# Mamba scan in a graph network on one core: B and C rows as sums of three BF16 parts, C read from PSUM, and GpSimd making the input of five of sixteen states

## The chip, the cores and the metric

The kernel runs on one core of one Trainium2 chip. The metric is the device time of one execution in microseconds, the median of the runs shown. Beside it stands one profiled execution, whose span and records are used for all readings of the trace.

## The reference, cut to what matters

Four graph layers follow each other on a graph of 3327 nodes with 256 features, each as `x = layernorm(x + layer(x, adj))`. The change lies in layer 1: one graph convolution, and then a Mamba block whose sequence is the nodes.

```python
h = jax.nn.relu(adj @ x @ gcn_w + gcn_b)
h = layernorm(h) * ln_g + ln_b
xz = h @ w_in                                  # 256 -> 2 x 512
xc, z = xz[:, :512], xz[:, 512:]
u = silu(causal_conv4(xc, conv_w) + conv_b)
dbc = u @ w_xp                                 # 512 -> 16 (dt) + 16 (B) + 16 (C)
dt = softplus(dbc[:, :16] @ w_dt + b_dt)
B, C = dbc[:, 16:32], dbc[:, 32:]
dA  = exp(dt[:, :, None] * A)                  # A = -exp(A_log): 512 x 16
dBu = dt[:, :, None] * B[:, None, :] * u[:, :, None]
def step(hst, inp):                            # hst: 512 channels x 16 states
    dAt, dBut, Ct = inp
    hst = dAt * hst + dBut
    return hst, hst @ Ct
_, ys = lax.scan(step, 0, (dA, dBu, C))
return ((ys + u * D_skip) * silu(z)) @ w_out
```

All inputs and the output are FP32.

## The kernel before

The nodes are padded to 26 tiles of 128. Layer 0 runs first (up to some 366 us), then layer 1, then two more layers; the change touches layer 1 alone.

In layer 1 the token axis is cut into chunks of 512 columns (`WC`): six whole ones and a last one of 256. The 512 channels lie as four groups (`NG`) of 128 partitions. For each chunk and each of the 16 states `s`:

- `rows(x, s)`: for each of the two rows B and C of the state, TensorE broadcasts the row over 128 partitions, by an FP32 product of a column of the identity with `dbc` (48 rows), into a PSUM tile `ps`; ScalarE copies it to an SBUF tile `row` (L324). Then ScalarE makes `dA` by four Exp activations, one a group (L328).
- `scan(x, s)`: VectorE multiplies `du` (dt times u, 2048 columns) by the B row into `db` (L336), runs four scans of 512 columns (L339), copies the last column of each into `carry` (L341), and multiplies the result `h` by the C row (L342).
- TensorE adds `h` over the states into four PSUM tiles `y` through a product with the identity (L393).

Round these lie other pieces of work, which the loop over chunks and states mixes in:

- `convolve()`, a generator that `pump()` advances once per state: the adjacency product for one later tile in three stretches of up to nine products (L204), then its projection by `gcn_w`, Relu, `stats`, `rstd_of` (ScalarE's Sqrt and VectorE's reciprocal, L72 and L73) and `standardize` (L81). Its inner function `rest` transposes the tile and writes it into `hT`.
- `head(c + 1)`, a generator advanced in the last nine states: projections to `xc`, the causal convolution on VectorE (L270, L273), Silu, `dbc`, and softplus in pieces for `dt` and `du`.
- `gate_input(c)`, once per chunk at state 6: four projections with Silu into `sz`.
- `gate` and `back` of the chunk before, after state 0: the skip and gate products, `w_out`, the residual into `X` with statistics, and GpSimd's four scalings of `X` (L370).

The program text gives the order only in part: a scheduler places the instructions of each engine into that engine's queue, and each queue is then worked off in order. Waits are on semaphores. Tiles come from pools with a fixed number of buffers; an instruction that writes a buffer waits until its last reader is done. The pools that matter here are `ps` (three PSUM banks shared by the projections, transposes, rows and `w_out`), the PSUM pool `l1q` with one bank for `cb` (the accumulator of `convolve`), four banks for `y`, and in SBUF `row` (3), `dA` (2), `db` (1) and `h` (2).

Of the kernel before, what the change touches and what calls it, by code (L numbers as in the profile page):

```python
# [9 lines left out]
F32 = mybir.dt.float32  # L10
BF16 = mybir.dt.bfloat16
# [6 lines left out]
P = 128  # L18
D = 256
EPS = 1e-5  # L20
JH = 13
JC = 9
WC = 512
DI = 512
NG = DI // P
# [15 lines left out]
def gnn_kernel(ctx: ExitStack, tc: tile.TileContext, n: int, a: dict, out: bass.AP):  # L41
# [28 lines left out]
    def rstd_of(dst, var):  # L70
        std = small.tile([P, var.shape[1]], F32, name="std")
        nc.scalar.activation(std, var, AF.Sqrt, bias=eps_t)  # L72
        nc.vector.reciprocal(dst, std)  # L73
# [52 lines left out]
    with tc.tile_pool(name="l01", bufs=1) as xpool:  # L126
# [30 lines left out]
        with tc.tile_pool(name="l1b", bufs=1) as wpool, tc.tile_pool(name="l1aw", bufs=1) as cwork, \  # L157
                tc.tile_pool(name="l1at", bufs=2) as atp, tc.tile_pool(name="l1c", bufs=2) as ch, \
                tc.tile_pool(name="l1t", bufs=3) as tmp, tc.tile_pool(name="l1s", bufs=2) as work, \
                tc.tile_pool(name="l1p", bufs=3, space=PSUM) as psum, \  # L160
                tc.tile_pool(name="l1q", bufs=1, space=PSUM) as cpsum, \
                tc.tile_pool(name="l1y", bufs=1, space=PSUM) as ypsum:
            gw = load(wpool, "gcn_w")
# [5 lines left out]
            def by_channel(name):  # L169
# [2 lines left out]
                return t  # L172

            g1, b1 = by_channel("ln1_g"), by_channel("ln1_b")
            w_in, conv_w, conv_b, w_xp, w_dt, b_dt, d_skip, w_out, A = (
                load(wpool, x) for x in
                ("w_in", "conv_w", "conv_b", "w_xp", "w_dt", "b_dt", "D_skip", "w_out", "A_log"))

            nc.scalar.activation(A, A, AF.Exp)
            nc.vector.tensor_scalar_mul(A, A, -1.0)  # L180
# [4 lines left out]
            R = DTR + 2 * DS  # L185
            nch = -(-npad // WC)
            tw = WC // P
            hTs, us, szs = {}, {}, {}

            def scratch():  # L190
                return tmp.tile([P, NG, 3 + WC], F32, name="t")

            def convolve():

                rest = None
                for it in range(nt):
                    cb = cpsum.tile([P, 2, D], F32, name="cb")
# [17 lines left out]
                    mt = cwork.tile([P, D], F32, name="mt")  # L215
# [4 lines left out]
                    h = cwork.tile([P, D], F32, name="h")  # L220
# [32 lines left out]
            def project(c, g, w):  # L253
                ps = psum.tile([P, WC], F32, name="ps")
                for k in range(2):
                    nc.tensor.matmul(ps[:, :w], w_in[:, k, g * P:(g + 1) * P], hTs[c][:, k, :w],
                                     start=(k == 0), stop=(k == 1))
                return ps[:, :w]

            def head(c):  # L260


                w = min(WC, npad - c * WC)
                xc = scratch()
                nc.vector.tensor_copy(xc[:, :, :3], last)
# [17 lines left out]
                dbc = ch.tile([R, WC], F32, name="dbc")  # L283
                nc.scalar.copy(dbc[:, :w], ps[:R, :w])
                yield None


                v, e, e1 = (scratch()[:, :, :w] for _ in range(3))
                for g in range(NG):
                    ps = psum.tile([P, WC], F32, name="ps")  # L290
                    nc.tensor.matmul(ps[:, :w], w_dt[:, g * P:(g + 1) * P], dbc[:DTR, :w],
                                     start=True, stop=True)
                    nc.scalar.activation(v[:, g, :], ps[:, :w], AF.Identity, bias=b_dt[:, g:g + 1])
                    nc.scalar.activation(e[:, g, :], ps[:, :w], AF.Abs, bias=b_dt[:, g:g + 1])
# [11 lines left out]
                yield dbc, dt, du  # L306

            def gate_input(c):
                w = us[c].shape[2]
                sz = szs[c] = ch.tile([P, NG, WC], F32, name="sz", bufs=1)[:, :, :w]  # L310
                for g in range(NG):
                    nc.scalar.activation(sz[:, g, :], project(c, NG + g, w), AF.Silu)

            def rows(x, s):

                dbc, dt, du = x
                w = dt.shape[2]
                bc = []
                for r in (DTR + s, DTR + DS + s):
                    ps = psum.tile([P, WC], F32, name="ps")  # L320
                    nc.tensor.matmul(ps[:, :w], ident[:R, r:r + 1].to_broadcast([R, P]), dbc[:, :w],  # L321
                                     start=True, stop=True)
                    row = work.tile([P, 1, WC], F32, name="row", bufs=3)
                    nc.scalar.copy(row[:, 0, :w], ps[:, :w])  # L324
                    bc.append(row[:, :, :w].to_broadcast([P, NG, w]))
# [3 lines left out]
                return bc, dA  # L329

            def scan(x, s, bc, dA):

                du = x[2]
                w = du.shape[2]
                db = work.tile([P, NG, WC], F32, name="db", bufs=1)[:, :, :w]
                nc.vector.tensor_mul(db, du, bc[0])  # L336
                h = work.tile([P, NG, WC], F32, name="h")[:, :, :w]
                for g in range(NG):
                    nc.vector.tensor_tensor_scan(h[:, g, :], dA[:, g, :], db[:, g, :], initial=carry[:, s, g:g + 1],  # L339
                                                 op0=ALU.mult, op1=ALU.add)  # L340
                nc.vector.tensor_copy(carry[:, s, :], h[:, :, w - 1])  # L341
                nc.vector.tensor_mul(h, h, bc[1])  # L342
                return h

            def gate(c, ys):
# [7 lines left out]
            def back(c):  # L353
# [10 lines left out]
                    nc.vector.tensor_add(X[:, it, :], X0[:, it, :], po)  # L364
                    stats(mv[:, i, :], X[:, it, :])
                rs = small.tile([P, tw], F32, name="rsc")
                rstd_of(rs[:, :m], mv[:, :m, 1])
                for i in range(m):
                    it = c * tw + i
                    nc.gpsimd.tensor_scalar(X[:, it, :], X[:, it, :], mv[:, i, 0:1], rs[:, i:i + 1],  # L370
# [9 lines left out]
            for c in range(nch):  # L380
                w = us[c].shape[2]
                ahead = None
                for s in range(DS):
# [646 lines left out]
```

## Time and profile before

| | |
|---|---|
| median of 3 runs | 4333.3 us (4333.17 to 4333.75) |
| profiled execution, its own time | 4330.06 us |
| its span | 4327.9 us |
| mean granted TensorE clock | 0.927 |
| layer 1 within the span | about 366 to 1815 us |

Engines are named PE (TensorE), PEld (its weight loads), DVE (VectorE), ACT (ScalarE), POOL (GpSimd) and SP (which issues the transfers). A row of a group reads: line, engine, operation, tile written and tiles read, shape, count, then busy time in us and the mean of one in ns, then the idle time of the engine just before these instructions and what ended it. A row of a windows table reads: stretch in us, its length, busy time of PE, PEld, DVE, ACT and POOL with instruction counts, the granted clock, the busy share of the DMA engines, and GB/s. A row of a wait list reads: engine, tile and line that waited, engine, tile and line that ended it, us in total, times, longest. An FP32 product is two matmul records in the trace.

### The profile page before, as it was taken

What the parts mean: (1) busy time and instruction counts of PE and PEld (TensorE: products, weight loads), DVE (VectorE), ACT (ScalarE), POOL (GpSimd) and SP (SyncE); (2) the same over time, 40 slices, a digit from 0 to 9 for tenths busy, and PEclk for the clock granted to TensorE, in tenths of its full rate; (3) what the DMA queues carried; (4) which work ended last, traced back from release to release, by engine and by line L of the source; (5) the groups of instructions that cost most, each with busy time, mean ns of one, the idle gap of its engine ahead of it and who ended that gap; (6) DMA issues with size and microseconds to landing.
All of it is one profiled execution on the core that took longest, in us unless ns stands there. A gap on an engine that the chain in (4) does not pass through costs nothing. (4 is left out here: it accounts for less than half of the span.)

```text
span 4327.9 us, 42860 instructions
## 1 busy us (share of the span) xinstructions
PE 3880.5 (90%) x15597; PEld 2791.7 (65%) x15597; DVE 2795.9 (65%) x6159; ACT 1731.7 (40%) x2826; POOL 276.6 (6%) x344
## 2 busy tenths in 40 slices
PE   8998999999999977799889999999868889888988
PEld 7886644444444433588767777777646767676767
DVE  1111588888888899688624444444158877787784
ACT  0001444444444544510033333333265656565652
POOL 0000000000000010133300000000000000000000
PEclk9998898989898988899969999999869999999999
DMA  5443211111111000044301111111101111111111
GB/s 180 136 141 98 68 37 32 37 32 32 32 32 32 21 0 0 21 159 152 131 16 48 48 53 59 48 48 49 32 0 51 41 46 40 46 40 46 41 45 37
DMA packets 67053, 239.33 MB, mean 55 GB/s; under 512 B 8434, under 2 KB 22770, under 8 KB 66690
## 3 DMA queue, kind: packets, MB, share of 16 engines
q1 hardware_dynamic: 66818, 236.37, 17.1%
q8 instruction: 127, 2.08, 0.2%
q14 instruction: 108, 0.88, 0.1%
HBM read 232.93 MB, written 3.41 MB: 55 GB/s over the span
## 5 line engine op out<-in xcount | busy, mean ns | idle before, releaser
L393 PE MATMUL y<-h,ident 128*128 128x512 f32 (+1 forms) x896 | 466.4, 671 | 91.3 <-DVE h L342 91.3
L339 DVE TENSOR_TENSOR_SCAN h<-dA,carry,db 128x512 f32<-128x512 f32 (+1 forms) x448 | 511.6, 1193 | 4.8 <-DVE db L336 0.5
L328 ACT ACTIVATE dA<-dt,A_log 128x512 f32<-128x512 f32 (+1 forms) x448 | 281.4, 684 | 350.8 <-DVE h L339 333.1
L393 PEld LDWEIGHTS y<-h,ident 128*128 128x128 f32 x896 | 192.2, 225 | 354.2 <-issue 206.4
L204 PE MATMUL cb<-X,at 128*128 128x256 f32 x1352 | 334.6, 403 | 26.9 <-ACT h L221 14.7
L204 PEld LDWEIGHTS cb<-X,at 128*128 128x128 f32 x1352 | 270.1, 203 | 113.7 <-issue 52.2
L122 PE MATMUL acc<-Xa,wt 128*128 128x256 f32 x1352 | 322.3, 391 | 19.3 <-ACT wt L120 18.9
L122 PE MATMUL acc<-X,wt 128*128 128x256 f32 x1352 | 310.1, 383 | 10.7 <-ACT wt L120 8.7
L107 PE MATMUL acc<-xa,at 128*128 128x257 f32 x1352 | 308.3, 381 | 0.0
L107 PE MATMUL acc<-Xf,at 128*128 128x256 f32 x1352 | 307.6, 379 | 0.0
L107 PE MATMUL acc<-X,at 128*128 128x256 f32 x1352 | 304.3, 379 | 0.0
L122 PEld LDWEIGHTS acc<-Xa,wt 128*128 128x128 f32 x1352 | 260.4, 196 | 67.3 <-ACT wt L120 31.9
L642 PE MATMUL ps<-kT,q 64*128 64x416 f32 x832 | 254.8, 595 | 54.2 <-ACT e L643 31.6
L549 PE MATMUL acc<-V,at 128*128 128x257 f32 x1352 | 294.2, 379 | 1.4 <-DVE at L546 1.4
L336 DVE TENSOR_TENSOR db<-du,row 128x2048 f32<-128x2048 f32 (+1 forms) x112 | 238.9, 2133 | 82.8 <-ACT row L324 82.6
L122 PEld LDWEIGHTS acc<-X,wt 128*128 128x128 f32 x1352 | 252.4, 190 | 59.5 <-ACT wt L120 27.3
L549 PEld LDWEIGHTS acc<-V,at 128*128 128x128 f32 x1352 | 255.8, 189 | 39.8 <-DVE at L546 1.8
L107 PEld LDWEIGHTS acc<-xa,at 128*128 128x128 f32 x1352 | 255.6, 191 | 37.5 <-issue 0.7
L96 ACT COPY xt<-ps 128x256 f32<-128x256 f32 x234 | 82.0, 373 | 491.3 <-PE ps L94 436.8
L107 PEld LDWEIGHTS acc<-X,at 128*128 128x128 f32 x1352 | 253.0, 190 | 32.3
L107 PEld LDWEIGHTS acc<-Xf,at 128*128 128x128 f32 x1352 | 251.4, 190 | 31.3
L321 PE MATMUL ps<-dbc,ident 48*128 48x512 f32 (+1 forms) x448 | 234.3, 637 | 20.3 <-ACT row L324 19.8
(273 smaller groups left out, 5698.6 us busy)
## 6 DMA issues: line engine op xcount, KB each, us to landing
at<-in_adjT SPq DMA_DIRECT2D x156, 576.0 KB, 3.7
at<-in_adjT SPq DMA_DIRECT2D x104, 832.0 KB, 4.4
at<-in_adjT SPq DMA_DIRECT2D x78, 512.0 KB, 3.5
xa<-in_x SPq DMA_DIRECT2D x1, 3328.0 KB, 12.7
xt<-in_xT SPq DMA_DIRECT2D x26, 128.0 KB, 3.9
out<-h SPq DMA_DIRECT2D x25, 128.0 KB, 1.7
w_in<-in_w_in SPq DMA_DIRECT2D x1, 1024.0 KB, 5.4
U<-in_U SPq DMA_DIRECT2D x2, 512.0 KB, 6.1
```

The source lines that it names most:

```text
L96: nc.scalar.copy(t, pt)
L107: nc.tensor.matmul(acc, at[:, j, :], rhs[:, j0 + j, :], start=(j0 + j == 0), stop=(j0 + j == nt - 1))
L122: nc.tensor.matmul(acc, wt[:, j, :], rhs[:, j0 + j, :], start=(j0 + j == 0), stop=(j0 + j == nt - 1))
L204: nc.tensor.matmul(acc, at[:, j % JC, :], X0[:, j, :], start=(j == 0), stop=(j == nt - 1))
L321: nc.tensor.matmul(ps[:, :w], ident[:R, r:r + 1].to_broadcast([R, P]), dbc[:, :w], start=True, stop=True)
L328: nc.scalar.activation(dA[:, g, :], dt[:, g, :], AF.Exp, scale=A[:, g, s:s + 1])
L336: nc.vector.tensor_mul(db, du, bc[0])
L339: nc.vector.tensor_tensor_scan(h[:, g, :], dA[:, g, :], db[:, g, :], initial=carry[:, s, g:g + 1], op0=ALU.mult, op1=ALU.add)
L393: nc.tensor.matmul(ys[g][:, :w], ident, h[:, g, :], start=(s == 0), stop=(s == DS - 1))
L549: nc.tensor.matmul(acc, at[:, j, :], V[:, j0 + j, :], start=(j0 + j == 0), stop=(j0 + j == nt - 1))
L642: nc.tensor.matmul(pl[:, :w], q[a:a + DA, :], kT[a:a + DA, c0:c0 + w], start=True, stop=True)
```

## The change

- `w_xp` is loaded into `w_sp`, with the B and C columns three times over and the dt columns last, so that `dbc` comes out with 112 rows: three equal copies of B and C, then dt.
- `head` makes `parts`, 96 rows in BF16: the first 32 rows are the rounded values, the next 32 the rounded remainder, the last 32 the remainder of that. Their sum is the FP32 row. This takes two subtractions on VectorE and four copies on ScalarE, in place of one copy.
- `rows` makes the B row by a BF16 product of a 96-row selector `three` with `parts`, which sums the three parts in PSUM. Only B is copied to SBUF.
- `scan` makes the C row in the same way, into a PSUM tile `C` with one buffer, and VectorE's second product reads it there. The `ps` pool shrinks from three banks to two for that.
- `db` is made in halves of two groups (three buffers of a half). For the states 1, 4, 7, 10 and 13 GpSimd makes both halves in `rows`; for the others VectorE makes them in `scan`.
- The carry copy moves from VectorE to ScalarE.
- In layer 1 `rstd_of` is replaced by `power` on GpSimd: add eps, then pow with -0.5.
- `gate_input` does one projection in each of the states 2 to 5.
- The tiles `m`, `mt` and `h` of `convolve` share one buffer.

```diff
+POOLED = (1, 4, 7, 10, 13)
...
-                tc.tile_pool(name="l1p", bufs=3, space=PSUM) as psum, \
+                tc.tile_pool(name="l1p", bufs=2, space=PSUM) as psum, \
...
+            BC = 2 * DS
+            w_sp = wpool.tile([P, NG, 3 * BC + DTR], F32, name="w_sp")
...
+            three = wpool.tile([3 * BC, BC], BF16, name="three")
+            for k in range(3):
+                nc.sync.dma_start(w_sp[:, :, k * BC:(k + 1) * BC], a["w_xp"][:, :, DTR:])
+                nc.vector.tensor_copy(three[k * BC:(k + 1) * BC, :], ident[k * BC:(k + 1) * BC, k * BC:(k + 1) * BC])
+            nc.sync.dma_start(w_sp[:, :, 3 * BC:], a["w_xp"][:, :, :DTR])
...
+            def power(rs, var):
+                nc.gpsimd.tensor_scalar(rs, var, EPS, None, op0=ALU.add)
+                nc.gpsimd.tensor_tensor(rs, rs, mhalf[:, :var.shape[1]], op=ALU.pow)
...
-                    rstd_of(rs, mv[:, 1:2])
+                    power(rs, mv[:, 1:2])
...
-                    nc.tensor.matmul(ps[:R, :w], w_xp[:, g, :], u[:, g, :],
+                    nc.tensor.matmul(ps[:3 * BC + DTR, :w], w_sp[:, g, :], u[:, g, :],
...
-                nc.scalar.copy(dbc[:, :w], ps[:R, :w])
+                parts = ch.tile([3 * BC, WC], BF16, name="parts")[:, :w]
+                nc.scalar.copy(parts, ps[:3 * BC, :w])
+                left = scratch()[:3 * BC + DTR, 0, :w]
+                nc.scalar.copy(left, ps[:3 * BC + DTR, :w])
+                nc.vector.tensor_sub(left[:3 * BC], left[:3 * BC], parts)
+                for k in (1, 2):
+                    nc.scalar.copy(parts[k * BC:(k + 1) * BC], left[k * BC:(k + 1) * BC])
+                nc.vector.tensor_sub(parts[2 * BC:], left[2 * BC:3 * BC], parts[2 * BC:])
...
-                for r in (DTR + s, DTR + DS + s):
-                    nc.tensor.matmul(ps[:, :w], ident[:R, r:r + 1].to_broadcast([R, P]), dbc[:, :w],
-                    row = work.tile([P, 1, WC], F32, name="row", bufs=3)
-                    nc.scalar.copy(row[:, 0, :w], ps[:, :w])
+                nc.tensor.matmul(pb, three[:, s:s + 1].to_broadcast([3 * BC, P]), parts, start=True, stop=True)
+                B = work.tile([P, 1, WC], F32, name="row", bufs=2)[:, :, :w]
+                nc.scalar.copy(B[:, 0, :], pb)
...
+                dbs = [work.tile([P, 2, WC], F32, name="db", bufs=3)[:, :, :w] for _ in range(2)]
+                if s in POOLED:
+                    for i in range(2):
+                        nc.gpsimd.tensor_tensor(dbs[i], du[:, 2 * i:2 * i + 2, :], B.to_broadcast([P, 2, w]), op=ALU.mult)
...
-                nc.vector.tensor_mul(db, du, bc[0])
+                C = cpsum.tile([P, 1, WC], F32, name="C")[:, :, :w]
+                nc.tensor.matmul(C[:, 0, :], three[:, DS + s:DS + s + 1].to_broadcast([3 * BC, P]), parts,
+                                 start=True, stop=True)
+                if s not in POOLED:
+                    for i in range(2):
+                        nc.vector.tensor_mul(db[i], du[:, 2 * i:2 * i + 2, :], B.to_broadcast([P, 2, w]))
...
-                nc.vector.tensor_copy(carry[:, s, :], h[:, :, w - 1])
-                nc.vector.tensor_mul(h, h, bc[1])
+                nc.scalar.copy(carry[:, s, :], h[:, :, w - 1])
+                nc.vector.tensor_mul(h, h, C.to_broadcast([P, NG, w]))
...
-                rstd_of(rs[:, :m], mv[:, :m, 1])
+                power(rs[:, :m], mv[:, :m, 1])
...
-                    if s == DS - 10:
-                        gate_input(c)
+                    if 2 <= s < 2 + NG:
+                        gate_input(c, s - 2)
```

More of the change, by code (lines that the diff above doesn't have):

```diff
@@ L174, in gnn_kernel @@
             g1, b1 = by_channel("ln1_g"), by_channel("ln1_b")
-            w_in, conv_w, conv_b, w_xp, w_dt, b_dt, d_skip, w_out, A = (
-                load(wpool, x) for x in
-                ("w_in", "conv_w", "conv_b", "w_xp", "w_dt", "b_dt", "D_skip", "w_out", "A_log"))
+            w_in, conv_w, conv_b, b_dt, d_skip, w_out, A = (
+                load(wpool, x) for x in ("w_in", "conv_w", "conv_b", "b_dt", "D_skip", "w_out", "A_log"))
             nc.scalar.activation(A, A, AF.Exp)
@@ L184, in gnn_kernel @@
             nc.vector.memset(last, 0.0)
-            R = DTR + 2 * DS
+            BC = 2 * DS
+            w_sp = wpool.tile([P, NG, 3 * BC + DTR], F32, name="w_sp")
+            w_dt = wpool.tile([3 * BC + DTR, DI], F32, name="w_dt")
+            nc.sync.dma_start(w_dt[3 * BC:, :], a["w_dt"])
+            three = wpool.tile([3 * BC, BC], BF16, name="three")
[3 more added lines that the diff above has]
+            nc.sync.dma_start(w_sp[:, :, 3 * BC:], a["w_xp"][:, :, :DTR])
+            mhalf = wpool.tile([P, 4], F32, name="mhalf")
+            nc.vector.memset(mhalf, -0.5)
             nch = -(-npad // WC)
@@ L214, in convolve @@
                         nc.tensor.transpose(tp[:, k * P:(k + 1) * P], m[:, k * P:(k + 1) * P], ident)
-                    mt = cwork.tile([P, D], F32, name="mt")
+                    mt = cwork.tile([P, D], F32, name="m")
                     nc.scalar.copy(mt, tp)
@@ L219, in convolve @@
                     nc.tensor.matmul(acc, one, gb, start=False, stop=True)
-                    h = cwork.tile([P, D], F32, name="h")
+                    h = cwork.tile([P, D], F32, name="m")
                     nc.scalar.activation(h, acc, AF.Relu)
@@ L280, in head @@
                 for g in range(NG):
-                    nc.tensor.matmul(ps[:R, :w], w_xp[:, g, :], u[:, g, :],
+                    nc.tensor.matmul(ps[:3 * BC + DTR, :w], w_sp[:, g, :], u[:, g, :],
                                      start=(g == 0), stop=(g == NG - 1))
-                dbc = ch.tile([R, WC], F32, name="dbc")
-                nc.scalar.copy(dbc[:, :w], ps[:R, :w])
+                parts = ch.tile([3 * BC, WC], BF16, name="parts")[:, :w]
[6 more added lines that the diff above has]
+                nc.vector.tensor_sub(parts[2 * BC:], left[2 * BC:3 * BC], parts[2 * BC:])
                 yield None
@@ L290, in head @@
                     ps = psum.tile([P, WC], F32, name="ps")
-                    nc.tensor.matmul(ps[:, :w], w_dt[:, g * P:(g + 1) * P], dbc[:DTR, :w],
+                    nc.tensor.matmul(ps[:, :w], w_dt[3 * BC:, g * P:(g + 1) * P], left[3 * BC:],
                                      start=True, stop=True)
@@ L305, in head, with gate_input @@
                 nc.vector.tensor_mul(du, dt, u)
-                yield dbc, dt, du
-            def gate_input(c):
+                yield parts, dt, du
+            def gate_input(c, g):
                 w = us[c].shape[2]
-                sz = szs[c] = ch.tile([P, NG, WC], F32, name="sz", bufs=1)[:, :, :w]
-                for g in range(NG):
-                    nc.scalar.activation(sz[:, g, :], project(c, NG + g, w), AF.Silu)
+                if g == 0:
+                    szs[c] = ch.tile([P, NG, WC], F32, name="sz", bufs=1)[:, :, :w]
+                nc.scalar.activation(szs[c][:, g, :], project(c, NG + g, w), AF.Silu)
             def rows(x, s):
-                dbc, dt, du = x
+                parts, dt, du = x
                 w = dt.shape[2]
-                bc = []
-                for r in (DTR + s, DTR + DS + s):
-                    ps = psum.tile([P, WC], F32, name="ps")
-                    nc.tensor.matmul(ps[:, :w], ident[:R, r:r + 1].to_broadcast([R, P]), dbc[:, :w],
-                                     start=True, stop=True)
-                    row = work.tile([P, 1, WC], F32, name="row", bufs=3)
-                    nc.scalar.copy(row[:, 0, :w], ps[:, :w])
-                    bc.append(row[:, :, :w].to_broadcast([P, NG, w]))
+                pb = psum.tile([P, WC], F32, name="ps")[:, :w]
+                nc.tensor.matmul(pb, three[:, s:s + 1].to_broadcast([3 * BC, P]), parts, start=True, stop=True)
+                B = work.tile([P, 1, WC], F32, name="row", bufs=2)[:, :, :w]
+                nc.scalar.copy(B[:, 0, :], pb)
                 dA = work.tile([P, NG, WC], F32, name="dA")[:, :, :w]
@@ L328, in rows, with scan @@
                     nc.scalar.activation(dA[:, g, :], dt[:, g, :], AF.Exp, scale=A[:, g, s:s + 1])
[L329 to L336, printed above, removed]
+                dbs = [work.tile([P, 2, WC], F32, name="db", bufs=3)[:, :, :w] for _ in range(2)]
+                if s in POOLED:
+                    for i in range(2):
+                        nc.gpsimd.tensor_tensor(dbs[i], du[:, 2 * i:2 * i + 2, :], B.to_broadcast([P, 2, w]), op=ALU.mult)
+                return B, dA, dbs
+            def scan(x, s, B, dA, db):
+                parts, dt, du = x
+                w = dt.shape[2]
+                C = cpsum.tile([P, 1, WC], F32, name="C")[:, :, :w]
[4 more added lines that the diff above has]
+                        nc.vector.tensor_mul(db[i], du[:, 2 * i:2 * i + 2, :], B.to_broadcast([P, 2, w]))
                 h = work.tile([P, NG, WC], F32, name="h")[:, :, :w]
                 for g in range(NG):
[L339 to L342, printed above, removed]
+                    nc.vector.tensor_tensor_scan(h[:, g, :], dA[:, g, :], db[g // 2][:, g % 2, :],
+                                                 initial=carry[:, s, g:g + 1], op0=ALU.mult, op1=ALU.add)
+                nc.scalar.copy(carry[:, s, :], h[:, :, w - 1])
+                nc.vector.tensor_mul(h, h, C.to_broadcast([P, NG, w]))
                 return h
```

## The prediction

> **What bounds the kernel now.** Part 1 of the page first: no engine is full over the whole span, so the Mamba stage has to be read by itself.
>
> ```profile
> PE 3880.5 (90%) x15597; PEld 2791.7 (65%) x15597; DVE 2795.9 (65%) x6159; ACT 1731.7 (40%) x2826; POOL 276.6 (6%) x344
> ```
>
> GpSimd's L370 runs once per chunk of 512 tokens, so its start times (735.16, 943.19, 1151.32, 1359.48, 1563.75, 1728.85, 1810.87) cut the stage into chunks. The windows table over these stretches (length, then busy time of PE, PEld, DVE, ACT, POOL, and the granted clock):
>
> ```profile
> 735.16:943.19 208.03, 191.18 (x521) 99.67 (x520) 182.94 (x170) 99.17 (x157) 9.06 (x5) 0.90 0.11 33
> 1359.48:1563.75 204.27, 174.63 (x454) 85.71 (x453) 183.72 (x168) 98.19 (x152) 9.07 (x4) 0.88 0.06 20
> 1563.75:1728.85 165.10, 133.83 (x286) 58.08 (x284) 162.06 (x158) 78.08 (x130) 13.02 (x4) 0.84 0.00 0
> 1728.85:1810.87 82.02, 60.29 (x194) 40.88 (x194) 72.36 (x105) 37.25 (x85) 10.62 (x5) 0.83 0.08 27
> ```
>
> A full chunk is 208.0 us; VectorE works 182.9 of it and idles 25.1. In the 165 us chunk, where the adjacency product has run out, VectorE works 98%. PE shows 191, but its stretches overlap in the pipeline and it often stands in front of VectorE's result (below, L393 waits for L342). So VectorE sets the pace and PE is close behind. The groups of lines over three chunks (735.16 to 1359.48):
>
> ```profile
> L339 DVE TENSOR_TENSOR_SCAN h<-dA,carry,db 128x512 f32<-128x512 f32 x193 | 235.5, 1269 | 2.9 <-DVE db L336 0.5
> L393 PE MATMUL y<-h,ident 128*128 128x512 f32 x385 | 209.6, 691 | 31.3 <-DVE h L342 31.3
> L342 DVE TENSOR_TENSOR h<-h,row 128x2048 f32<-128x2048 f32 x48 | 109.9, 2290 | 3.7
> L336 DVE TENSOR_TENSOR db<-du,row 128x2048 f32<-128x2048 f32 x48 | 109.7, 2285 | 51.2 <-ACT row L324 51.2
> L321 PE MATMUL ps<-dbc,ident 48*128 48x512 f32 x192 | 106.4, 667 | 0.0
> L341 DVE COPY carry<-h 128x4 f32<-128x4 f32 x48 | 8.1, 169 | 1.1
> ```
>
> Per state VectorE does one product (2.3), four scans (4.8), a carry copy and another product (2.3). The waits of VectorE in the first of these chunks:
>
> ```profile
> DVE db L336 <- ACT row L324: 17.1, 6, 6.6
> DVE u L270 <- ACT t L268: 2.7, 2, 2.1
> DVE u L349 <- PE y L393: 1.4, 1, 1.4
> DVE rs L73 <- ACT std L72: 1.3, 1, 1.3
> ```
>
> Two stretches make 12.9 of the 17.1: 6.33 at 802.6 (the row waits behind gate_input's burst of four projections) and 6.57 at 893.0 (behind four dt projections and their eight activations). The last question is what GpSimd costs beside VectorE: L370's four instructions at 1563.75 (start, duration, each from a narrow timeline), and two groups of the page's kind.
>
> ```profile
> 1563.75 3.17 POOL L370 TENSOR_SCALAR X<-X,mvc,rsc 128x256 f32<-128x256 f32 x1 [195.19 <-DVE rsc L73]
> 1569.35 4.97 POOL L370 TENSOR_SCALAR X<-X,mvc,rsc 128x256 f32<-128x256 f32 x1
> 1574.31 2.46 POOL L370 TENSOR_SCALAR X<-X,mvc,rsc 128x256 f32<-128x256 f32 x1
> L874 POOL TENSOR_TENSOR rs<-rs,mhalf 128x1 f32<-128x1 f32 x52 | 30.3, 583 | 4.3
> L879 POOL TENSOR_TENSOR t<-X,ln_b 128x256 f32<-128x256 f32 x26 | 18.9, 726 | 15.0 <-DVE h L891 15.0
> ```
>
> The same form (L567) takes 1.23 us at 1904.4. Under scans alone (1574.31) it takes 2.46, half speed; the 4.97 lay for 3.9 us under two VectorE products and got almost nowhere. VectorE's four scans beside it took 4.91 against 4.81, so VectorE hardly pays.
>
> **What the Trainium skill says.** "GPSIMD Engine Reference", sections Specifications and Architecture: GpSimd's SBUF interfaces are shared with VectorE, with contention against VectorE instructions that have two SBUF inputs. The trace agrees (1.23 against 2.46 to 4.97). Same page, section "Elementwise — side-by-side cycle accounting": a tensor_tensor add over 2048 FP32 columns takes 4497 ns; with L879's 726 ns for 256 that is 2.10 ns a column. No run here shows 1024 columns; my estimate is 0.726 + 768 x 2.10 = **2.34 us a half**. "VectorE: DVE Perf Modes", section "The perf-mode tier table": an FP32 tensor_tensor runs at 1x from SBUF and with a PSUM operand alike; the trace has 742 ns with a PSUM input (L349) beside 739 without (L273). "FP8 and Floating Point Precision", section TensorE Precision Notes: true FP32 takes four passes through the array; here each FP32 matmul is two records 0.43 us apart, so I take 0.86 / 4 = 0.22 us for a BF16 one.
>
> **The change, part by part, per full chunk.**
> VectorE's work: five of sixteen db products go to GpSimd, -5 x 2.285 = -11.4. Sixteen carry copies go to ScalarE, -16 x 0.169 = -2.7. Five reciprocals go, -0.75. Eleven db products become two halves (the 128x1024 form of L336 takes 1.220): 11 x (2.440 - 2.285) = +1.7. Two subtractions over 512 columns (from 1.220 and 2.285: 1.04 ns a column, 0.69 each) = +1.4. The product with C reads PSUM: 0, by L349 and L273 within 0.1 x 16 either way. Sum -11.8: 182.9 becomes **171.1**.
> PE: 64 FP32 records of L321 (27.5 us at 0.43) become 32 BF16 ones (7): some 20 us less, 22 at clock 0.90. ScalarE: -16 C copies (0.58), +16 carry copies (near 0.3, as std), +3 copies of parts, gate's silu now switches tables four times, but the Sqrt switches go (39 table loads before rows, 25 for Sqrt in the stage before; the built order shows 80 in all against 93). It stays near half busy.
>
> VectorE's waits: of the 25.1 the two long row stretches should go, as projections are spread one per state and PE has 22 us more. New ones come. I walked one chunk in the built order with the durations above; where VectorE stands still:
> (1) back() puts add, pow and four L370 scalings on GpSimd, ahead of the next tile's own add and pow. VectorE's standardize (L81) now waits for that pow, with state 2's scans queued behind it, and PE's transposes with state 3's rows behind those. From mvc: add and pow 0.9 (late, two db halves block them), 4 x 1.23, add and pow 0.9, against 2.5 us of VectorE work: **6.3**.
> (2) The other three standardizes: pow right after aggr, 1.0 and 0.4; in the third, both halves of state 10 stand ahead of it in GpSimd's queue: **4.5**.
> (3) The halves. Half 0 may start when the B row is there and the state two before has been scanned. VectorE then has product with C (one SBUF input: GpSimd runs free), a db half and two scans before it needs it, 6 us. State 4's row comes 3.4 us late on ScalarE (carry, dA, two table loads, silu): stall 1.3. State 7's row stands on PE behind y of state 5 and on ScalarE behind eight steps, 6.5 us late: stall **5.5**. Half 1 has five scans and a db half, 6 us, of which half speed gives 2.6: covered. States 1, 10 and 13: covered.
> (4) Exp of softplus 0.6. The carry copy on ScalarE waits for the scan's end, but so does the dA queued behind it: 0. One C buffer: C follows y on PE, 4.1 us after the product's end, and VectorE has at least 4.7 until it wants C: 0. Two ps buffers for three, with one row a state fewer: 0, up to 3 if PE stands.
> Sum 19.6. Chunk: 171.1 + 19.6 = **190.7** against 208.1, -17.4.
>
> Over the stage: the first chunk has no back(), so (1) does not arise: -20. Three chunks like the one above: -52. The chunk from 1359 (183.7 busy): -16. The chunk from 1563: no tiles, so only (3): busy -11.2, waits +2: -9.5. The half chunk: -6. The start: three more DMA issues on SP's queue (w_xp landed in one DMA of 96 KB in 4.5 us; now four pieces, 0.45 us an issue, ahead of the adjacency tiles) and a longer uncovered head for chunk 0 (two subtractions, three copies): +4, between 0 and 10. Sum **-99**. The profiled execution took 4330.1 us (span 4327.9), so 4231; the median of the runs stands 3.2 above it: **4234**.
>
> **Rivals.** *More gain.* The built order knows no contention, but state 7's row may come earlier than I walk, and (2) may fall under work. With 5 us of waits left, a chunk is 176: -32 for five chunks, -12 and -6 after: 4160 to 4200. For it: the last full chunk runs VectorE at 98%. Against it: (1) cannot be hidden.
> *No change.* Under scans GpSimd gets nothing; each of ten halves costs VectorE its whole 2.34, and (1) and (2) stay: 171 + 23 + 12 = 206. L370 at 2.46 speaks against it; that a two-stream product asks more of the port speaks for it. 2 us a chunk: 4325.
> *Slower.* A half costs GpSimd far more than 2.34 by itself: the trace shows no GpSimd instruction with a broadcast operand or over 256 columns. Some seven halves a chunk are uncovered, so each further us costs 7 a chunk, and the 17.4 is gone at 2.5 more: the point is a half of **4.8 us**. At 6 us: 25.6 - 17.4 = +8 for five chunks, +10 after: 4380. Against it stand L879 and the page's figure.
> *PE bound.* If PE paced, its 22 us per chunk would be the gain: 4210, on the same side.
>
> **How the numbers follow.** About 0.2% is what a measurement of this kernel can tell from no change. The walk, 4200 to 4280: 0.58. More gain: 0.18. Between 4280 and 4324: 0.04. Within 0.2%: 0.06. Slower: 0.14. Faster is then 0.80. The range goes from 4165, the deep end of "more gain", to 4340, a half near the deciding point; it leaves out 0.04 below and 0.12 above.
>
> **What would show it.** Right: chunk stretches near 191 us; VectorE near 171 in each; a wait of VectorE's L81 for GpSimd's pow of about 6 us once a chunk; GpSimd's db halves of 2.3 to 5 us; BF16 row records near 0.22 us apart. Wrong: halves over 5 us with scans waiting for them several us each; C's product over 2.4 us; scans well over 1.27 us; a granted clock below 0.88; or chunks of 208 with waits on PE.

## The result: slower by 0.6%

The changed kernel takes 4359.4 us (4353.0 to 4365.2) where the kernel before takes 4333.2: 1.0062 times the time, 95% interval 1.0045 to 1.0079. Foretold were 4234, in a range of 4165 to 4340. The profiled execution took 4365.2 us (span 4363.3), against 4330.1: 35 us, where the medians differ by 26.

The sums over the whole span hide what happened. Part 1 of the page of the changed kernel:

```profile
PE 3731.7 (86%) x15373; PEld 2755.1 (63%) x15373; DVE 2807.5 (64%) x6074; ACT 1674.6 (38%) x2800; POOL 472.0 (11%) x480
```

VectorE lost 85 instructions and gained 12 us of busy time. The windows table of the changed kernel, cut at the starts of GpSimd's scalings (L399, L370 before), shows it by chunk. The columns are length, then busy time of PE, PEld, DVE, ACT, POOL, the granted clock, DMA:

```profile
737.11:945.60 208.49, 167.65 (x488) 95.60 (x488) 184.40 (x156) 90.67 (x151) 40.17 (x25) 0.87 0.11 33
945.60:1153.24 207.64, 163.49 (x488) 91.87 (x488) 184.40 (x156) 90.44 (x151) 40.20 (x25) 0.89 0.11 33
1360.58:1570.31 209.73, 148.74 (x386) 75.63 (x387) 186.58 (x156) 92.81 (x152) 40.09 (x25) 0.84 0.04 11
1570.31:1738.25 167.94, 110.11 (x244) 51.19 (x242) 161.92 (x145) 73.63 (x132) 34.97 (x16) 0.80 0.00 0
1738.25:1835.02 96.77, 59.10 (x165) 40.41 (x165) 73.13 (x98) 33.28 (x82) 17.87 (x15) 0.68 0.05 18
```

PE did what was foretold (191.2 to 167.7 us busy, some 22 less forecast). VectorE did not: five products fewer, and 184.4 us busy instead of 182.9; 171.1 was forecast. A chunk is as long as before. The 35 us that the profiled executions differ by come from elsewhere: by these markers the three full chunks stand at +0.5, -0.5 and -0.8, the next at +5.5, then +2.8, the half chunk +14.8, the start +2.0, and everything after the Mamba stage +11.3. Groups of lines over three chunks (737.11 to 1360.58) show which VectorE instructions grew:

```profile
L368 DVE TENSOR_TENSOR_SCAN h<-dA,carry,db 128x512 f32<-128x512 f32 x192 | 264.5, 1419 | 15.1 <-POOL db L353 14.6
L371 DVE TENSOR_TENSOR h<-h,C 128x2048 f32<-128x2048 f32 x48 | 109.4, 2279 | 16.5 <-PE C L361 12.1 <-ACT carry L370 4.0
L365 DVE TENSOR_TENSOR db<-du,row 128x1024 f32<-128x1024 f32 x66 | 91.8, 1398 | 7.8 <-ACT row L346 7.7
L353 POOL TENSOR_TENSOR db<-du,row 128x1024 f32<-128x1024 f32 x30 | 82.0, 2758 | 363.4 <-ACT row L346 247.2 <-DVE du L330 116.1
```

A scan has the shape it had and takes 1.42 us, not 1.27. A db half takes 1.40; the same form took 1.22 in the half chunk of the kernel before. The product with C, of the same length as the db product of before, has not grown (2.28). GpSimd's half takes 2.76 in the mean, against the estimate of 2.34. Narrow timelines of the changed kernel (start, duration) show two of its pairs of halves. For the second pair, the line x2 is both halves and the line at 860.21 is the second one by itself:

```profile
788.51 2.39 POOL L353 TENSOR_TENSOR db<-du,row 128x1024 f32<-128x1024 f32 x1 [16.22 <-ACT row L346]
790.87 2.40 POOL L353 TENSOR_TENSOR db<-du,row 128x1024 f32<-128x1024 f32 x1
790.94 3.40 DVE L368 TENSOR_TENSOR_SCAN h<-dA,carry,db 128x512 f32<-128x512 f32 x1 [4.87 <-POOL db L353]
857.87 5.74 POOL L353 TENSOR_TENSOR db<-du,row 128x1024 f32<-128x1024 f32 x2 [31.68 <-ACT row L346]
860.21 3.40 POOL L353 TENSOR_TENSOR db<-du,row 128x1024 f32<-128x1024 f32 x1
857.07 2.29 DVE L371 TENSOR_TENSOR h<-h,C 128x2048 f32<-128x2048 f32 x1 [0.81 <-ACT carry L370]
859.27 2.08 DVE L365 TENSOR_TENSOR db<-du,row 128x1024 f32<-128x1024 f32 x1
861.39 3.30 DVE L368 TENSOR_TENSOR_SCAN h<-dA,carry,db 128x512 f32<-128x512 f32 x1
```

The half that starts at 788.51 has VectorE waiting for it, and takes 2.39. The next takes 2.40 although a scan is issued 0.07 us after it; that scan takes 3.40 = 1.27 + 2.13, almost the length of the half: it stood still until the half was done. At 857.87 a half starts in the middle of a product with C, and the product keeps its 2.29. VectorE's own db half behind that product takes 2.08 instead of 1.21: it stands until GpSimd's first half is done (860.27). GpSimd's second half, which starts while VectorE's is under way, takes 3.40 instead of 2.40, and the scan behind it 3.30 instead of 1.27. So the two engines hold each other up in turn, the later instruction standing, and VectorE stands in some of its instructions only. Since a stalled instruction counts as busy, no view of waits shows this; it appears only as a longer mean in the groups of lines, GpSimd's 2.76 among them.

VectorE's real waits in the chunk 737.11 to 945.60:

```profile
DVE m L82 <- POOL rs L204: 9.2, 4, 6.8
DVE h L368 <- POOL db L353: 4.9, 1, 4.9
DVE h L371 <- PE C L361: 3.8, 3, 2.0
DVE db L365 <- ACT row L346: 3.0, 1, 3.0
DVE h L371 <- ACT carry L370: 1.3, 3, 0.8
```

### The profile page after: what moved, and what is told of

It is laid out like the page before. It is cut to its first block, busy times and chain, and to the rows that moved or that the text cites. A ratio compares the mean times of both kernels' runs of the same rounds, so it can differ in the third digit from the quotient of the medians.

```text
span 4363.3 us, 42422 instructions
## 1 busy us (share of the span) xinstructions
PE 3731.7 (86%) x15373; PEld 2755.1 (63%) x15373; DVE 2807.5 (64%) x6074; ACT 1674.6 (38%) x2800; POOL 472.0 (11%) x480
## 5 line engine op out<-in xcount | busy, mean ns | idle before, releaser
L422 PE MATMUL y<-h,ident 128*128 128x512 f32 (+1 forms) x896 | 477.6, 687 | 185.7 <-DVE h L371 185.7
L368 DVE TENSOR_TENSOR_SCAN h<-dA,carry,db 128x512 f32<-128x512 f32 (+1 forms) x448 | 578.0, 1333 | 33.4 <-POOL db L353 28.2
L422 PEld LDWEIGHTS y<-h,ident 128*128 128x128 f32 x896 | 206.0, 238 | 433.5 <-DVE h L371 236.4
L220 PE MATMUL cb<-X,at 128*128 128x256 f32 x1352 | 343.8, 407 | 48.0 <-ACT m L237 33.7
L371 DVE TENSOR_TENSOR h<-h,C 128x2048 f32<-128x2048 f32 (+1 forms) x112 | 238.0, 2125 | 43.8 <-PE C L361 29.6
L353 POOL TENSOR_TENSOR db<-du,row 128x1024 f32<-128x1024 f32 (+1 forms) x70 | 179.3, 2582 | 782.5 <-ACT row L346 537.2
```

Source lines behind the costliest of these rows:

```text
L353: nc.gpsimd.tensor_tensor(dbs[i], du[:, 2 * i:2 * i + 2, :], B.to_broadcast([P, 2, w]), op=ALU.mult)
L368: nc.vector.tensor_tensor_scan(h[:, g, :], dA[:, g, :], db[g // 2][:, g % 2, :], initial=carry[:, s, g:g + 1], op0=ALU.mult, op1=ALU.add)
L371: nc.vector.tensor_mul(h, h, C.to_broadcast([P, NG, w]))
L422: nc.tensor.matmul(ys[g][:, :w], ident, h[:, g, :], start=(s == 0), stop=(s == DS - 1))
```

## The experiments

Theory *shared port*: a GpSimd product with two SBUF inputs holds up VectorE's instructions with two SBUF inputs, so what VectorE is spared comes back in its scans. Rival *waits*: the halves pay, and the new waits (pow, C, carry) eat it. Rival *layout*: scans are longer because db lies in two tiles or C in PSUM. The ratios below are to the kernel before, with 95% intervals.

**No pooled states.** `POOLED = ()`, nothing else.

> The changed kernel with POOLED empty: VectorE makes all db products, in halves; everything else of the change stays. Theory 'shared port' (a GpSimd product with two SBUF inputs holds up VectorE's instructions with two SBUF inputs, so what VectorE is spared it pays back): scans back from 1.42 us to 1.27, halves from 1.40 to 1.22, VectorE busy in a full chunk 182 to 183.5 us in spite of 10 halves more, the wait for GpSimd's db (4.9) gone; chunk about 200, total 4305 to 4335. Rival 'waits' (the halves pay, and the time is lost in new waits for pow, C and carry): VectorE 184.4 + 12.2 = 196.6 busy, chunk about 215, total near 4400. Rival 'layout' (scans are longer because db lies in two tiles or C in PSUM): scans stay at 1.42, total near 4400 too.

Measured: 4272.7 us, 0.9857 (0.9843 to 0.9872), faster than before by 60 us. One chunk of its windows table:

```profile
920.36:1114.43 194.07, 163.02 (x488) 91.18 (x488) 179.94 (x166) 90.19 (x151) 14.01 (x14) 0.91 0.12 36
```

Two of its groups of lines over three chunks (726.11 to 1309.67):

```profile
L368 DVE TENSOR_TENSOR_SCAN h<-dA,carry,db 128x512 f32<-128x512 f32 x192 | 233.7, 1264 | 0.0
L365 DVE TENSOR_TENSOR db<-du,row 128x1024 f32<-128x1024 f32 x96 | 114.7, 1210 | 4.8 <-ACT row L346 4.8
```

and VectorE's largest wait in the chunk from 920.36:

```profile
DVE m L82 <- POOL rs L204: 8.7, 4, 6.7
```

Scans are back at 1.26, with db still in two tiles and C still in PSUM: *layout* is out. VectorE makes ten halves more and is busy 4.5 us less. With ten halves of 1.21 taken off, it would be busy 167.8; the changed kernel shows 184.4, so each half on GpSimd cost VectorE 16.6 / 10 = 1.66 us to spare it 1.21. VectorE's idle time fell too, from 24.1 to 14.1, mostly where it waited for GpSimd's db (4.9) and for C (3.8, none in this chunk). The gain is larger than the theory had foretold (chunk 194, not 200). With the pow on GpSimd, as here, the pooling alone costs 4359.4 - 4272.7 = 87 us, and the rest of the change gains 60.

**Added work, two inputs.** The kernel before, plus GpSimd products that nobody reads (L334 below; L342 is the db product and L345 the scan, L336 and L339 in the kernel before):

```
+ if s in (1, 4, 7, 10, 13) and w == WC:
+     junk = X[:, nt - 4:, :].rearrange("p (a b) d -> p a (b d)", a=2)
+     for i in range(2):
+         nc.gpsimd.tensor_tensor(junk, du[:, 2*i:2*i+2, :],
+                                 row0[:, :, :w].to_broadcast([P, 2, w]), op=ALU.mult)
```

> The kernel before, with work added: for states 1, 4, 7, 10 and 13 of each full chunk GpSimd makes du x B row in two halves (128x1024, two SBUF inputs) into rows of X that are written over later; nobody reads them. Shared port: scans from 1.27 to about 1.40 us on average with some over 3, VectorE busy per chunk 183 + 10 to 15, total 4370 to 4410. Layout (stretch comes from half tiles of db or from PSUM): scans 1.27, total within 5 us of before.

Measured: 4440.7, 1.0238 (1.0223 to 1.0253), and VectorE 202.6 us busy in a full chunk where it was 182.9: +19.6 for ten halves. Both are above what was expected (4370 to 4410, and 10 to 15 us). A full chunk of its windows table:

```profile
752.83:982.41 229.58, 198.41 (x521) 101.56 (x520) 202.57 (x170) 100.20 (x155) 46.03 (x14) 0.87 0.10 30
```

Its timeline is read below, beside that of two kernels close to it.

**Added work, one input.** The same place and size, with `tensor_scalar(junk, du half, row0[:, 0, 0:1], ...)`.

> As the kernel with added two-input products, but GpSimd's extra instruction is a tensor_scalar over the same 128x1024 of du times one value per partition of the row: the same place, size and output, one input stream fewer. Shared port, by number of inputs: scans stay at 1.27 us and GpSimd's own instruction gets longer (from about 4.9 without contention to 6 or more, as the 256-column form goes from 1.23 to 2.46); total within 8 us of before. Rival, any GpSimd work stretches VectorE: scans 1.35 to 1.4, total 4370 or more.

Measured: 4369.0, 1.0080 (1.0065 to 1.0095). Scans rose to 1.33, between the two theories' numbers, and the total is within 1 us of the rival's least. A full chunk:

```profile
738.38:952.04 213.66, 193.49 (x520) 99.72 (x519) 189.61 (x170) 98.68 (x155) 48.95 (x15) 0.89 0.11 32
```

**Added two-input work, with VectorE's own product taking its row from PSUM** in those five states, so that this product has one SBUF input (L337, L345 and L348 are the half, the product and the scan here):

```
- bc.append(row[...])
+ bc.append(ps.rearrange("p (a w) -> p a w", a=1)[...])   # pooled states' B row only
```

> The kernel before with the added two-input halves on GpSimd, and VectorE's own db product of those five states reading the B row from PSUM instead of SBUF (one SBUF input); the row's PSUM bank is then held longer. Theory, an instruction with two SBUF inputs on either engine keeps the other engine's out until it ends: with the product out of the way the first half runs beside it at once (about 2.4 us) and the product stays at 2.28; the four scans behind it take 4.81 + about 2 us for one half, not 8.77 for two; VectorE busy in a full chunk from 202.6 to about 193 to 195, total 4385 to 4410 where the version with both inputs in SBUF took 4441. Rival, the stretch goes by how busy the memory is and not by the number of SBUF inputs: scans stay near 8.8 us for four, VectorE busy 202, total 4435 or more.

Measured: 4419.1, 1.0194 (1.0177 to 1.0211), 9 us above the theory's range and 16 below the rival's, so the total does not decide; the timeline does. One state of each in a timeline, first the kernel with both inputs in SBUF:

```profile
805.93 7.62 POOL L334 TENSOR_TENSOR X<-du,row 128x1024 f32<-128x1024 f32 x2 [27.28 <-ACT row L324]
805.82 2.29 DVE L342 TENSOR_TENSOR db<-du,row 128x2048 f32<-128x2048 f32 x1 [0.29 <-ACT row L324]
808.22 8.77 DVE L345 TENSOR_TENSOR_SCAN h<-dA,carry,db 128x512 f32<-128x512 f32 x4
```

then the one whose product reads PSUM:

```profile
803.82 5.71 POOL L337 TENSOR_TENSOR X<-du,row 128x1024 f32<-128x1024 f32 x2 [27.29 <-ACT row L324]
803.71 2.29 DVE L345 TENSOR_TENSOR db<-du,ps 128x2048 f32<-128x2048 f32 x1 [0.29 <-ACT row L324]
806.11 6.86 DVE L348 TENSOR_TENSOR_SCAN h<-dA,carry,db 128x512 f32<-128x512 f32 x4
```

and the one with one-input GpSimd instructions, a pair and then its second instruction by itself:

```profile
756.60 8.06 POOL L334 TENSOR_SCALAR X<-du,row 128x1024 f32<-128x1024 f32 x2 [9.15 <-ACT row L324]
758.88 6.29 DVE L345 TENSOR_TENSOR_SCAN h<-dA,carry,db 128x512 f32<-128x512 f32 x4
761.60 3.06 POOL L334 TENSOR_SCALAR X<-du,row 128x1024 f32<-128x1024 f32 x1
761.93 2.07 DVE L345 TENSOR_TENSOR_SCAN h<-dA,carry,db 128x512 f32<-128x512 f32 x1
```

Four scans take 4.81 undisturbed. Behind a two-input VectorE product that started 0.11 earlier, GpSimd's pair had to wait for it (7.62), and both halves then fell on the scans: 8.77 = 4.81 + 2 x 1.98. With one input of the product in PSUM and nothing else changed, the pair takes 5.71, the product keeps its 2.29, and the scans take 6.86: one half fewer falls on them, as the theory had it to 0.1 us. VectorE's busy time in a full chunk fell from 202.6 to between 194.9 and 196.7. That the number of SBUF inputs decides on VectorE's side is shown by this; the rival, memory load, had 8.8 for the scans.

On GpSimd's side it is a matter of degree. The one-input instruction holds one scan for 0.80 (2.07 for 1.27) of its own 3.06 us and lets the next pass; over a chunk VectorE pays 6.7 us for ten of them (189.6 against 182.9), a third of what two-input ones cost (19.6). Why it holds a scan for a part only is open.

**Scalings later.** The changed kernel, with back()'s four scalings written after state 4 instead of after its pow.

> The changed kernel with back()'s four scalings on GpSimd issued after state 4 instead of right after its pow; all else as changed. If the wait of the standardize for its pow behind the scalings costs what it shows (6.75 us a chunk, five chunks): chunks of 201, total 4359 - 5 x 6.3 = 4328. If it is absorbed by another wait (VectorE then stands for C or for a row): 4350 to 4360, with VectorE's idle per chunk still near 24.

Measured: 4359.7, 1.0062 (1.0048 to 1.0076): the changed kernel's own time. The scheduler put the scalings back where they were (736.80): every engine has the same instructions in the same order as in the changed kernel. The edit was none, and tells only how well a time repeats (4359.4 and 4359.7).

**The tiles' root back on ScalarE and VectorE**, halves kept: `power(rs, mv[:, 1:2])` becomes `rstd_of(rs, mv[:, 1:2])` in convolve.

> The changed kernel, pooled halves kept, with only the tiles' reciprocal root back on ScalarE and VectorE. Prices the wait behind the scalings on GpSimd (the version that issued the scalings later had been given the same order of instructions on GpSimd by the scheduler, and the same time). If it costs what it shows: VectorE's wait 9.2 becomes 1.3, four reciprocals 0.6, chunk 200.5, total 4359 - 5 x 7.3 = 4323. If another wait takes its place: above 4345.

Measured: 4320.0, 0.9976 (0.9968 to 0.9984), as expected to 3 us; chunks of 197.6 to 201. So the wait behind the scalings, with the smaller ones for pow, did cost what it showed, and without it the changed kernel is 0.2% faster than the one before. The halves still cost: e1 below differs from this in POOLED alone and is 52 us faster.

**Without pooled states, in four forms.**

```
c1  POOLED = (), one db product of 128x2048, row in 3 buffers, rstd_of for the tiles
c2  the same, but power for the tiles, and back()'s scalings by nc.vector
e1  POOLED = (), halves on VectorE, rstd_of for the tiles
e2  e1, and head's four dt projections in two states, starting one state earlier
```

> All db products on VectorE as one instruction over 128x2048, row with three buffers again, and the tiles' reciprocal root made by ScalarE and VectorE as before the change (back() keeps pow on GpSimd); everything else of the change stays. From the version with all halves on VectorE (chunk 194.1, 4272.7): whole products -2.2, the waits for pow 8.7 become about 1.3, four reciprocals +0.6: chunk 185, total 4272.7 - 5 x 9 = 4228. Rival (PE paces once VectorE is quicker: PE busy 163 of 194 in that version, y waits less): VectorE's idle moves to C, row or y, chunk 190 or more, total 4250 to 4270.

> As the version with whole products on VectorE and three row buffers, but the tiles' pow stays on GpSimd and back()'s four scalings go to VectorE (four of 0.41 us). The wait of 6.7 behind the scalings is then 2 to 2.5 (add and pow of back, then of the tile), the others stay near 2: chunk 194.1 - 2.2 - 4.5 + 1.6 = 189, total near 4248. If ScalarE's extra steps in the version with its own root cost more than 1.3 us a chunk, this one is the faster of the two; else the slower by 15 to 20.

> POOLED empty with halves on VectorE (the version at 4272.7, chunk 194.1), and the tiles' reciprocal root back on ScalarE and VectorE. The waits for pow (8.7 in a chunk) become about 1.3, four reciprocals 0.6: chunk 187, total 4272.7 - 5 x 7 = 4238; in the version with whole products the same step brought nothing, since a wait for a row of 6.3 behind the dt projections took its place. Rival: here too, chunk 193, total 4265 to 4280.

> The same, and head(c + 1) starts one state earlier and makes its four dt projections and eight activations in two states, two and two. If the row's wait behind that burst is what is left: 3 to 6 us a chunk less than the version without it, 4215 to 4230. If the wait only moves (rows stand behind something else in ScalarE's queue): within 8 us of it.

Measured: c1 4281.6, 0.9878 (0.9863 to 0.9893); c2 4302.5, 0.9936 (0.9923 to 0.9950); e1 4268.2, 0.9849 (0.9836 to 0.9863); e2 **4261.9**, 0.9833 (0.9819 to 0.9846). All four stand 30 to 55 us above what the sum of removed waits gave: other waits took their place, and in c1 more than the rival allowed. c2 is 21 us slower than c1, where its second branch had 15 to 20. In c1 the wait for pow is gone, and the largest of VectorE's idle times in a chunk is now, in its timeline,

```profile
1073.99 2.29 DVE L360 TENSOR_TENSOR db<-du,row 128x2048 f32<-128x2048 f32 x1 [6.31 <-ACT row L346]
```

the row that stands behind the dt projections' activations on ScalarE. In e1, with halves, the 8.7 for pow became these in the chunk from 918.20:

```profile
DVE h L371 <- PE C L361: 4.1, 2, 2.2
DVE u L289 <- ACT t L287: 2.2, 1, 2.2
DVE db L365 <- ACT row L346: 2.1, 1, 2.1
DVE bnst L78 <- ACT m L237: 2.0, 1, 2.0
```

The chunk went from 194.1 to 191.4 only. The same edit was worth 39 us with pooled halves and 4.5 without, which the totals alone cannot tell from noise. The whole product costs VectorE less than two halves (2.29 against 2.42) and still c1 is the slower, by 13 us: in these chunks no wait for a row is over 2.1 in e1, and one is 6.3 in c1. Splitting the dt projections brought 6 us, within the 8 that the rival allowed. e2 has the lowest median measured, 71 us below the kernel before, but its interval overlaps that of e1.

**One part of the change alone.** The kernel before, with gate_input's projections in states 2 to 5.

> The kernel before with one edit of the change alone: gate_input's four projections in states 2 to 5 instead of all in state 6. If the row wait of 6.3 us behind the burst is what it costs: VectorE's wait for rows 17.1 becomes about 11, chunk 202, total 4333 - 5.5 x 6 = 4300. If PE is too full to fit the rows in (191 of 208 busy), the wait moves to other states: 4325 to 4335; four table loads for one in a chunk (ScalarE has half its time free) 0.

Measured: 4340.7, 1.0020 (1.0013 to 1.0026): slightly slower, and 6 us above the range of the second branch. VectorE's waits for rows stayed (19.6 in 8 stretches, longest 7.4, in a chunk of 208.9). With PE 190 of 209 busy, spreading the burst moved the row's wait and did not end it.

**The rows' cost on PE put back.** No pooled states, and each of the 32 BF16 row products issued four times.

> POOLED empty with halves on VectorE, and each of the 32 BF16 row products of a chunk issued four times over (the last one counts), so that the rows cost PE about what the FP32 ones did. If PE's 20 to 22 us are what took VectorE's waits from 25 to 14 a chunk: PE busy from 163 to about 185, waits for rows and C back, chunk 203 to 208, total 4320 to 4335. If the gain came from C in PSUM, two-half db buffers and the carry copy on ScalarE, and PE has slack: PE's busy time rises as much and the chunk stays at 194 to 197, total 4273 to 4288.

Measured: 4334.7, 1.0004 (0.9995 to 1.0012): the gain of 60 us is gone in the total. A chunk of its windows table:

```profile
943.77:1143.68 199.91, 176.04 (x585) 97.44 (x584) 181.31 (x167) 90.82 (x151) 14.22 (x15) 0.97 0.12 35
```

The B rows' products in its groups of lines over three chunks:

```profile
L345 PE MATMUL ps<-parts,three 96*128 96x512 bf16 x192 | 52.0, 394 | 1.8 <-ACT hT L251 1.8
```

VectorE's two largest waits in that chunk:

```profile
DVE db L367 <- ACT row L347: 7.2, 3, 5.0
DVE h L373 <- PE C L363: 4.2, 1, 4.2
```

VectorE's own time has hardly changed (181.3); its waits for rows and C are back. The chunks are 200 to 203, below the 203 to 208 expected: PE's busy time rose by 13 to 15 us, not 22, and the chunk by about half of that. So within the chunks some half of the gain is gone, with half of the 28 us by which PE's busy time had fallen put back. The rest of the 60 is spread over the start (the first scaling starts at 740.9, 726.1 without the repeats), the last chunks and the half chunk, and the order of instructions shifts with the repeats, so not all of it need be PE's. Nor does this run separate PE's total work from the later arrival of each single row. That C in PSUM, the buffers and the carry copy bring the gain by themselves is refuted.

## Why the prediction was wrong

**The step that failed** is in the first sum: "five of sixteen db products go to GpSimd, -5 x 2.285 = -11.4", with "VectorE hardly pays" behind it. Without pooled states and with the change's other edits, the prediction's own terms give VectorE 171.1 + 10 x 1.22 = 183. Its waits are then 19.6 - 6.8 = 12.8, or some 9 if the time put down to state 10's halves goes too. That is a chunk of 192 to 196; measured were 180 of work and a chunk of 194. So in a full chunk the other terms together held to 2 us. In this term's place the runs showed +4.5 us: 12.1 spared, 16.6 paid. Of the prediction's own signs of being wrong, "scans well over 1.27 us" came. The error was to carry over what L370 showed. L370 is a one-input tensor_scalar of 256 columns that cost four scans 0.1 us; a two-input product of 1024 columns costs them 1.98. The reading had one side of it: the L370 of 4.97 lay behind two VectorE products with both inputs in SBUF.

The Trainium skill had it. The prediction rested on "GPSIMD Engine Reference" (section Specifications), which says that there is contention and not who stands. "SBUF — State Buffer", says more, in the sections "SBUF: two separate sides" and "Who interferes with whom": a VectorE instruction with two SBUF inputs and a GpSimd instruction that reads SBUF exclude one another, the first to start keeps the port for its whole length, and the other blocks fully. With two-input products on GpSimd the runs agree: 2.40 for the half that came first and 3.40 for the scan behind it, 3.40 for the half that came second, and 8.77 against 6.86. The one-input form differs: a scan beside it stood for 0.80 of 3.06 us, not for the whole.

**The rivals.** *No change* was nearest. It had "each of ten halves costs VectorE its whole 2.34": measured 1.66, and 1.98 under scans alone. Its picture, in which GpSimd gets nothing under scans, was half of what happens: each engine stands for the other in turn. *Slower* had the right side and a wrong mechanism: a half takes 2.39 by itself, far from 4.8. *PE bound* named a source of the gain that the other edits bring: with half of PE's time put back, the total is that of the kernel before.

**Waits, 19.6 forecast, 24.1 measured in the chunk from 737.** (1) standardize behind the scalings: 6.3 forecast, 6.8. (2) the other standardizes: 5.9 forecast, 2.4. (3) state 7's halves 5.5, measured 4.9; state 4's 1.3, measured 0; a row 0, measured 3.0. (4) C and the carry copy, costed at 0, measured 3.8 and 1.3. The sum is 4.5 us short of what was measured, a third of the error in VectorE's work (184.4 - 171.1 = 13.3).

**The half chunk** was to gain 6 and lost 14.8. Timelines of the changed kernel, GpSimd, ScalarE and VectorE:

```profile
1738.25 5.55 POOL L399 TENSOR_SCALAR X<-X,mvc,rsc 128x256 f32<-128x256 f32 x4
1743.77 2.48 POOL L353 TENSOR_TENSOR db<-du,row 128x512 f32<-128x512 f32 x2
1746.28 0.37 ACT L346 COPY row<-ps 128x256 f32<-128x256 f32 x1 [7.78 <-POOL db L353]
1746.78 1.22 DVE L371 TENSOR_TENSOR h<-h,C 128x1024 f32<-128x1024 f32 x1 [6.72 <-ACT carry L370]
```

With 256 tokens a state is half as long, but the scalings are not. The pooled halves wait behind them and hold a row buffer; ScalarE, which works its queue in order, stands for that buffer with the carry copy queued behind; and VectorE's product, which overwrites h, stands for the carry copy. The step "the carry copy waits for the scan's end, but so does the dA queued behind it: 0" looked at what is behind the copy and not at what is ahead of it. Without pooled states this chunk is 84.1 us, 2.1 above before. Not all of the 14.8 is the change's: in the run with the scalings written later, which has the same instructions in the same order, the chunk took 91.0 us, at a granted clock of 0.79 where this execution shows 0.68. Some 6 us are of this execution, and some 7 of the pooled halves.

**Start and end.** The first chunk was to gain 20 and the start to lose 4; the first scaling starts 2.0 later than before (9 earlier without pooled states). After the stage 11.3 us were lost where none were costed. The first product with V starts 49.4 us after the last back's first scaling, not 44.9. The four runs built on the kernel before have 45.9 to 47.0 here, so some 2 to 4 us are left for the change. A likely cause is that the load of layer 2's weights is issued after the last pow on GpSimd (1834.94), where it was issued 3.3 us ahead of the first scaling before; no run isolates it. From that product to the end the changed kernel took 2478.9 us and the kernel before 2472.1, with the same instructions. The four runs built on the kernel before, which have these too, took 2476.8 to 2482.5, so these 7 us need not be the change's.

## What to carry to other kernels

Before work moves from VectorE to GpSimd, count the SBUF inputs on both sides: two against two meant here that the engines take turns, and then the move pays only if VectorE stands for less than it is spared (1.66 against 1.21 us here). Read the cost in the mean duration of unmoved instructions, since a stalled instruction shows as busy and no table of waits has it. And price relief on the second-busiest engine by taking it away again: PE did not look like the limit, and with half of its relief taken back the total was that of the kernel before.

## What the runs showed of the hardware

- A GpSimd product over 128x1024 FP32 with two SBUF inputs takes 2.39 to 2.41 us when it starts first, with a VectorE scan or db half issued after it.
- A VectorE scan issued behind it stands for nearly the whole half (3.40 for 1.27), and a GpSimd half issued behind a VectorE db half stands in turn (3.40 for 2.40); a VectorE product with one input in PSUM does not stand at all (2.29 beside such a half).
- A one-input GpSimd tensor_scalar of the same size holds a scan for 0.80 of 3.06 us: 0.67 a piece of VectorE's time over a chunk, against 1.96 for two inputs.
